# Attention with a conditioning token: other PSUM banks in the opening, and another order of sums, maxima and residual loads in the last two steps

## The chip, the cores and the metric

The kernel runs on one core of a Trainium2 chip. The metric is the device time of one execution in microseconds (us). TensorE multiplies matrices into PSUM, VectorE and ScalarE read PSUM, GpSimd works between tiles in SBUF, and the SP queue issues nearly all DMAs. PSUM has 8 banks of 128 x 512 float32 here, numbered 0 to 7.

## The reference, cut to what matters

```python
# x: (8, 512, 512), cond: (8, 512); 16 heads of 32
Q, K, V = heads(x @ Wq.T + bq), heads(x @ Wk.T + bk), heads(x @ Wv.T + bv)
tQ, tK  = heads(cond @ Wq.T + bq), heads(cond @ Wk.T + bk)
scores  = einsum('bhqd,bhkd->bhqk', Q + tQ, K + tK) / sqrt(32)
attn    = softmax(scores)
return x + einsum('bhqk,bhkd->bhqd', attn, V)      # heads put side by side again
```

All is float32. `x` comes back in as the residual; the bias of V is added to the residual, since the weights of a row sum to one.

## The kernel before, in words

The work is cut into T = 32 steps: step t is batch `t // 4` and a group of four heads `t % 4` (128 columns). Each step has four quarters. In quarter i of step t:

- `exponentials(t, i)` (L542) makes the scores of 128 keys by 512 queries for four heads, one bank each: first L547 puts minus the row maximum of each query in the bank, then L550 adds K times Q. ScalarE takes the exponential of each bank (L561) into tiles `es[t, i, pair]`.
- `row_max(t + 1, i + 1)` (L469) makes the scores of the next step the other way around, 128 queries by 512 keys (L486), for the row maxima on VectorE (L477 for one bank, L495 for two). `denominators` (L499) lets ScalarE run over the same banks once more (L505, tile `dead`) for the sums over keys. So such a bank comes free only when ScalarE is through with it.
- A third part differs by quarter: projections of a later batch (`project_pair`: `first_products`, `other_products`; L393 for q and k, L390 for v; seven products of half blocks in two banks, put together by VectorE at L431 to L447), or the product of the exponentials with V (`times_v`, L566, into one bank).

When all four quarters of maxima of a step are there, `split_max` (L513) has GpSimd cut them into three bfloat16 numbers (L519 to L522), and `transpose_max` (L526) turns those on TensorE (L531) and copies them out (L537, tile `maxT`), for the L547 of the next step.

The engines TensorE, ScalarE, VectorE and GpSimd issue their instructions in the order in which the program writes them (a schedule by hand). The SP queue alone is filled by a planner. Which banks a quarter uses is read from a table, `TURNS` (L83): each row is an order of the 8 banks. `banks(i)` is the i-th bank of the current row; `exponentials` takes places 0 to 3 and `row_max` places 4 to 7. `advance()` goes to the next row. Rows 0 to 7 serve the loop in turn, rows 8 to 11 steps 29 and 30 (`row(i)`), and rows 12 to 16 the opening (L716 to L737), where the maxima of step 0 and the first of step 1 are made between the projections of batch 0. Row 15 serves its quarter 3 of step 0 (`row_max(0, 3)`, `first_products("k", ...)` at places 3 and 2), row 16 the first quarter of step 1 (`row_max(1, 0)`, `transpose_max` at place 1, `other_products` at places 0 and 2).

Residuals: `load_residual(t)` (L153) loads a tile `xr` on SP, in four DMAs, and GpSimd adds the bias (L169). Tile `xr` has three buffers. For the last step the output is turned on TensorE, so its residual comes in another layout, in one DMA (L165), and before the change in the same three buffers. A buffer is free when `send` (L619) has used it: VectorE turns the product (L622), GpSimd multiplies by the reciprocals of the sums (L623) and adds the residual (L624), and SP writes out (L627).

Steps 29, 30 and 31 are written out after the loop. There is no projection left, so a product with V is made in pieces: `part_of` (L742) makes some quarters of it in a bank, ScalarE copies it out (L756, or L750 for later pieces), and GpSimd adds later pieces to the first (L751). Steps 30 and 31 have no `denominators`: their sums over keys are made from `es`. `sum_of` (L821) adds quarters 0 and 1 (L824) or one more quarter (L826) for one pair of heads, on VectorE or GpSimd, and `times_ones` (L574, L576) adds over the partitions on TensorE. `send_parts` (L764) takes the reciprocals (L766) and sends a step that was made in pieces.

Of the kernel before, what the change touches and what calls it, by code (L numbers as in the profile page):

```python
# [9 lines left out]
F32 = mybir.dt.float32  # L10
# [7 lines left out]
def kernel(  # L18
# [38 lines left out]
    nc = tc.nc  # L57
    P = 128
# [6 lines left out]
    NS = S // P  # L65
    NC = D // P
# [10 lines left out]
    op = ctx.enter_context(tc.tile_pool(name="op", bufs=2))  # L77
# [20 lines left out]
        (7, 4, 2, 3, 5, 6, 0, 1),  # L98
        (7, 4, 0, 1, 5, 6, 2, 3),
        (2, 3, 4, 7, 5, 6, 0, 1),  # L100
        (2, 3, 4, 7, 0, 1, 5, 6),
        (4, 7, 5, 6, 2, 3, 0, 1),
    ]
    turn = [0]

    def banks(i, n=1):

        j = TURNS[turn[0]][i]
        if n == 1:
            return psum[:, j, :]  # L110
        k = TURNS[turn[0]][i + 1]
        return psum[:, j : k + 1 : k - j, :]
# [19 lines left out]
    BL = 32  # L132
    NB = S // BL
# [13 lines left out]
    xr = {}  # L147
# [5 lines left out]
    def load_residual(t):  # L153

        b, g = divmod(t, G)
        if turned_by_vector(t):
            xr[t] = op.tile([P, NB, BL], F32, tag="xr", name=f"xr_{t}", bufs=3)
            for h in range(HG):
                nc.sync.dma_start(
                    xr[t][h * BL : (h + 1) * BL], spread(x[b], g * P + h * BL)  # L160
                )
            bias = bvs[:, g, :].unsqueeze(1).broadcast_to([P, NB, BL])
        else:
            xr[t] = op.tile([P, NS, P], F32, tag="xr", name=f"xr_{t}", bufs=3)
            nc.sync.dma_start(  # L165
                xr[t], x[b].rearrange("(c p) d -> p c d", p=P)[:, :, g * P : (g + 1) * P]
            )
            bias = bvb[:, g * P : (g + 1) * P].unsqueeze(1).broadcast_to([P, NS, P])
        nc.gpsimd.tensor_tensor(xr[t], xr[t], bias, ALU.add)  # L169
# [134 lines left out]
    def turn_x(n):  # L304
        b, cc = divmod(n, NC)
        if b >= B:
            return
        if cc == 0:
            xT[b] = xtp.tile([P, NC, S], F32, tag="xT", name=f"xT_{b}")
        nc.vector.transpose(xT[b][:, cc, :], xs[n].rearrange("p f i -> p (f i)"))  # L310
        load_block(n + NC)
# [157 lines left out]
    def row_max(t, qc):  # L469
        if t >= T:  # L470
            return
        open_max(t)
        for j in range(HG):
            row_scores(t, qc, j, banks(HG + j))
        if t < T - 2:
            for j in range(2):
                nc.vector.tensor_reduce(  # L477
                    nmax[t][:, qc, j : j + 1, 0], banks(HG + j), AX.X, ALU.max, negate=True
                )
        else:  # L480
            row_max_of(t, qc, 0, banks(HG, 2))
        row_max_of(t, qc, 1, banks(HG + 2, 2))
# [43 lines left out]
    def transpose_max(t, bank, copy=nc.vector.tensor_copy):  # L526
        if t >= T:
            return
        pt = bank.bitcast(BF16)
        for qc in range(NS):  # L530
            nc.tensor.transpose(  # L531
                pt[:, qc * P : (qc + 1) * P],
                split[t % 2][:, qc, :, :].rearrange("p h e -> p (h e)"),
                identb,
            )
        maxT[t] = op.tile([P, S], BF16, tag="maxT", name=f"maxT_{t}")
        copy(maxT[t], pt[:, :S])  # L537
# [36 lines left out]
    def times_ones(of, pt, start, stop):  # L574
        for j in range(HG):
            nc.tensor.matmul(  # L576
                pt[j * HD : (j + 1) * HD, :],
                ones[:, :HD],
                of[j // 2][:, j % 2, :],
                start=start,  # L580
                stop=stop,
            )
# [84 lines left out]
    def bank(i):  # L667
        return psum[:, i, :]
# [71 lines left out]
    parts = {}  # L740

    def part_of(t, pt, of, between=None):  # L742

        for k, kc in enumerate(of):
            if k and between:
                between()
            times_v(t, kc, pt, of)
        if t in parts:
            p = op.tile([P, S], F32, tag="dead", name=f"part_{t}_{of[0]}")
            nc.scalar.copy(p, pt)  # L750
            nc.gpsimd.tensor_tensor(parts[t], parts[t], p, ALU.add)  # L751
        else:
            if not parts:
                parts["all"] = stage.tile([P, NC, D], F32, tag="w", name="parts")
            parts[t] = parts["all"][:, t % NC, :]
            nc.scalar.copy(parts[t], pt)  # L756
# [7 lines left out]
    def send_parts(t, den):  # L764
        rec = op.tile([P, NB, 1], F32, tag="recs", name=f"recs_{t}")
        nc.vector.reciprocal(rec, den)  # L766
        send(t, parts[t], rec)

    for t in range(T - 3):
        b, r = divmod(t, G)  # L770

        exponentials(t, 0)
        row_max(t + 1, 1)
        of = ((t - 1) // G + 1, (t - 1) % G)
        dens = lambda: denominators(t + 1, 1)
        if t:
            project_pair("q", *of, dens, nothing, 1 if r % 2 else (0, 3))
        else:
            first_products("v", 0, 0, dens, nothing, 3)
            turn_x(NC + 2)  # L780
        turn_x(t + NC + 3)
        advance()

        exponentials(t, 1)
        row_max(t + 1, 2)
        dens = lambda: denominators(t + 1, 2)
        if t:
            dens()
            weighted(
                t - 1, banks(0), banks(1), lambda: combine_x(b + 1, r) if r < 2 else None  # L790
            )
        else:
            dens()
            other_products("v", 0, 0, nothing, nothing, (1, 0))
        advance()

        exponentials(t, 2)
        row_max(t + 1, 3)
        split_max(t + 1)
        dens = lambda: denominators(t + 1, 3)  # L800
        if t:
            project_pair("k", *of, dens, nothing, 1 if r % 2 else (0, 3))
        else:
            first_products("v", 0, 1, dens, nothing, 3)
            combine_x(1, 0)
        load_residual(t + 1)
        advance()

        exponentials(t, 3)
        row_max(t + 2, 0)  # L810
        dens = lambda: denominators(t + 2, 0)

        def small():
            transpose_max(t + 1, banks(2 if r % 2 else 1))

        project_pair("v", *of, dens, small, 1 if r % 2 else (0, 2))
        advance()
# [3 lines left out]
    def sum_of(t, to, kc, on, prs=range(NP)):  # L821
        for pr in prs:
            if kc == 1:
                on.tensor_tensor(to[pr], es[t, 0, pr], es[t, 1, pr], ALU.add)  # L824
            else:
                on.tensor_tensor(to[pr], to[pr], es[t, kc, pr], ALU.add)  # L826

    def room_for_sums(t):
        a = stage.tile([P, NC, D], F32, tag="w", name=f"acc_{t}")
        return [a[:, pr * 2 : pr * 2 + 2, :] for pr in range(NP)]  # L830

    def row(i):
        turn[0] = 8 + i

    t = T - 3
# [2 lines left out]
    row_max(t + 1, 1)  # L838
    part_of(t - 1, banks(0), [0, 1])
    load_residual(t + 1)  # L840
    row(1)
    exponentials(t, 1)
    row_max(t + 1, 2)
# [8 lines left out]
    den = denominators_of(t - 1, banks(1))  # L852
# [6 lines left out]
    t = T - 2  # L859
# [2 lines left out]
    row_max(t + 1, 1)  # L862
    apart = masked(t - 1)
    part_of(t - 1, banks(0), [2])
    load_residual(t + 1)
    row(1)
    exponentials(t, 1)
    row_max(t + 1, 2)
    part_of(t - 1, banks(0), [3])
    spread_sums(apart, banks(1))  # L870
    den = denominators_of(t - 1, banks(1))
    row(2)
    exponentials(t, 2)
    row_max(t + 1, 3)
    acc = room_for_sums(t)
    sum_of(t, acc, 1, nc.gpsimd, [0])
    split_max(t + 1)
    part_of(t, banks(0), [0])
    send_parts(t - 1, den)

    exponentials(t, 3, (1, 2, 3, 4))
    sum_of(t, acc, 1, nc.vector, [1])
    part_of(
        t, bank(5), [1, 2], lambda: transpose_max(t + 1, bank(0), nc.vector.tensor_copy)
    )
    sum_of(t, acc, 2, nc.vector)
    sum_of(t, acc, 3, nc.vector)

    t = T - 1
    exponentials(t, 0, (6, 7, 1, 2))  # L890
    part_of(t - 1, bank(3), [3])
    exponentials(t, 1, (0, 4, 5, 6))
    pv = bank(7)
    times_v(t, 0, pv)
    exponentials(t, 2, (1, 2, 3, 0))
    times_v(t, 1, pv)
    times_ones(acc, bank(4), True, True)
    den = parts["all"][:, t % NC, :].rearrange("p (f e) -> p f e", e=BL)
    acc2 = room_for_sums(t)
    sum_of(t, acc2, 1, nc.vector)  # L900
    nc.vector.transpose(den.rearrange("p f e -> p (f e)"), bank(4))
    send_parts(t - 1, den[:, :, 0:1])
    exponentials(t, 3, (5, 6, 1, 2))
    times_v(t, 2, pv)
    pd = bank(3)
    times_ones(acc2, pd, True, False)
    times_ones([es[t, 2, pr] for pr in range(NP)], pd, False, False)
    times_ones([es[t, 3, pr] for pr in range(NP)], pd, False, True)
# [5 lines left out]
    two = [slice(0, HS), slice(HS, S)]  # L914
    nc.vector.tensor_copy(oT[:, two[0]], pv[:, two[0]])
    nc.scalar.copy(oT[:, two[1]], pv[:, two[1]])
    pi, po = bank(0), [bank(5), bank(1)]
    untranspose(den, pi)
    rec = op.tile([P, NS, HG, 1], F32, tag="rec", name="rec")
    nc.vector.reciprocal(  # L920
# [52 lines left out]
```

## Time and profile before

| | |
|---|---|
| median of 3 runs | 741.74 us (741.56 to 742.1) |
| the profiled execution | 741.48 us |
| its span in the profile | 739.6 us |
| TensorE, matmuls | busy 729.2 us (99%) |
| ScalarE | 620.6 us (84%) |
| VectorE | 535.2 us (72%) |
| GpSimd | 185.3 us (25%) |
| granted TensorE clock | 0.998 |

The span runs from the first instruction to the last end; all times of the text are counted from its start. In a line of the timeline stand the start, the duration, the engine and line, what is written and read, and how many instructions were merged; brackets hold the idle time before and what ended it. PE is TensorE, ACT ScalarE, DVE VectorE, POOL GpSimd. In a list of waits stand the waiting engine and line, what it waited for, us in total, times, and the longest. A matmul that waits while others are in flight is shown as a longer busy time, not as idle time, so distances between starts tell more than busy time does.

### The profile page before, as it was taken

The page shows a single profiled execution, that of the slowest core. Times are in us where ns is not written, and L with a number is a line of the kernel's source. Part 1 is how long each engine was busy: PE and PEld are TensorE (multiplying, and loading weights), DVE is VectorE, ACT ScalarE, POOL GpSimd, SP SyncE. Part 2 cuts the span into 40 slices and gives each one's busy share as a digit, 9 for nine tenths or more (in the row PEclk, how much of TensorE's full clock was granted, in tenths as well). Part 3 has the DMA queues.
Part 4 walks back from the last instruction along what each step waited for, and adds up shares of the span by engine and source line. Part 5 has one row for each costly group of instructions (what it writes and reads, how often), then busy time and mean ns, then how long its engine had stood idle before and what let it go on. Part 6 is the DMA issues. An engine that isn't in the chain of part 4 may idle for free.

```text
span 739.6 us, 15126 instructions
## 1 busy us (share of the span) xinstructions
PE 729.2 (99%) x5432; PEld 406.5 (55%) x5432; DVE 535.2 (72%) x845; ACT 620.6 (84%) x1546; POOL 185.3 (25%) x283
## 2 busy tenths in 40 slices
PE   9999999999999999999999999999999999999987
PEld 6566555655555565555566555566555556555422
DVE  3588777777777876777776877677676776766776
ACT  2478888988988988988989898898898898898664
POOL 3721211222211122221122221122222112222273
PEclk9999999999999999999999999999999999999999
DMA  8511212222212212221222221222111011111012
GB/s 261 85 30 29 37 24 43 34 39 45 44 26 33 44 30 44 44 33 27 43 33 40 44 43 23 37 41 33 29 31 16 15 30 29 30 29 25 7 29 43
DMA packets 194270, 29.63 MB, mean 40 GB/s; under 512 B 190986, under 2 KB 192010, under 8 KB 194196
## 3 DMA queue, kind: packets, MB, share of 16 engines
q1 hardware_dynamic: 193616, 28.01, 22.6%
q8 instruction: 42, 0.69, 0.4%
q10 hardware_dynamic: 580, 0.68, 0.3%
q14 instruction: 32, 0.26, 0.1%
HBM read 20.27 MB, written 8.39 MB: 39 GB/s over the span
## 4 chain that ended last, share of the span: by engine, by line
PE 94%; POOL 1%; DVE 1%; ACT 1%; DMA 1%; issue 1%; SPq 0%; DVEq 0%; POOLq 0%; ACTq 0%
PE psum L393 25%; PE psum L566 15%; PE psum L486 15%; PE psum L550 14%; PE psum L390 14%; PE psum L547 6%; PE psum L337 2%; PE psum L531 1%; DVE nmax L495 1%; PE psum L253 1%; ACT e L561 1%; PE psum L576 1%; DMA x<-in_x_dram 1%; DMA xr<-in_x_dram 0%; PE psum L298 0%
## 5 line engine op out<-in xcount | busy, mean ns | idle before, releaser
L505 ACT ACTIVATE dead<-psum,nmax 128x512 f32<-128x512 f32 x480 | 326.9, 700 | 8.1 <-DVE nmax L477 5.4
L561 ACT ACTIVATE e<-psum 128x512 f32<-128x512 f32 x512 | 264.4, 604 | 76.5 <-PE psum L550 76.5
L477 DVE TENSOR_REDUCE nmax<-psum 128x1 f32<-128x512 f32 x240 | 154.7, 686 | 144.6 <-PE psum L486 144.6
L495 DVE TENSOR_REDUCE nmax<-psum 128x2 f32<-128x1024 f32 x136 | 164.7, 1216 | 10.4 <-PE psum L486 9.1
L623 POOL TENSOR_TENSOR res<-res,recs 128x512 f32<-128x512 f32 x31 | 32.4, 1047 | 443.5 <-DVE res L622 443.5
L486 PE MATMUL psum<-kT,qT 32*128 32x512 f32 x1024 | 137.2, 601 | 0.1
L550 PE MATMUL psum<-qT,kT 32*128 32x512 f32 x1024 | 133.0, 588 | 0.0
L566 PE MATMUL psum<-e,v 128*32 128x512 f32 x1024 | 120.8, 597 | 0.0
L505 ACT ACTIVATION_READ_ACCUMULATOR dead<-psum,nmax 128x1 f32 x480 | 104.6, 218 | 0.0
L486 PEld LDWEIGHTS psum<-kT,qT 32*128 32x128 f32 x1024 | 58.3, 183 | 57.0 <-ACT dead L505 20.6
L566 PEld LDWEIGHTS psum<-e,v 128*32 128x32 f32 x1024 | 26.4, 110 | 65.4 <-issue 37.0
L547 PE MATMUL psum<-maxT,onesb 3*128 3x512 bf16 x512 | 52.7, 384 | 0.3 <-ACT dead L505 0.3
L550 PEld LDWEIGHTS psum<-qT,kT 32*128 32x128 f32 x1024 | 51.1, 185 | 2.4 <-issue 0.2
L390 PE MATMUL psum<-wc_v,xc 128*128 128x256 f32 x192 | 49.5, 380 | 0.3 <-ACT e L561 0.2
L547 PEld LDWEIGHTS <-onesb 3*128 3x128 bf16 x512 | 13.5, 91 | 62.1 <-issue 52.5
L393 PE MATMUL psum<-xc,wc_q 128*128 128x256 f32 x180 | 46.2, 379 | 0.0
L393 PE MATMUL psum<-xc,wc_k 128*128 128x256 f32 x180 | 46.2, 379 | 0.0
L624 POOL TENSOR_TENSOR res<-res,xr 128x512 f32<-128x512 f32 x31 | 40.4, 1303 | 2.4
L169 POOL TENSOR_TENSOR xr<-xr,bvs 128x512 f32<-128x512 f32 x31 | 39.3, 1268 | 2.8 <-DMA xr<-in_x_dram 2.6
L390 PEld LDWEIGHTS psum<-wc_v,xc 128*128 128x128 f32 x192 | 36.3, 190 | 6.0 <-ACT e L561 1.1
L390 PE MATMUL psum<-wT_v,xT 128*128 128x256 f32 x128 | 38.7, 405 | 0.0
L393 PEld LDWEIGHTS psum<-xc,wc_q 128*128 128x128 f32 x180 | 34.2, 190 | 4.7
(156 smaller groups left out, 790.7 us busy)
## 6 DMA issues: line engine op xcount, KB each, us to landing
xr<-in_x_dram SPq DMA_DIRECT2D x124, 64.0 KB, 2.4
out_dram<-res SPq DMA_DIRECT2D x124, 64.0 KB, 2.0
x<-in_x_dram SPq DMA_DIRECT2D x112, 64.0 KB, 2.4
w_q<-in_L_cond_Wq_dram SPq DMA_DIRECT2D x4, 256.0 KB, 4.6
w_k<-in_L_cond_Wk_dram SPq DMA_DIRECT2D x4, 256.0 KB, 3.6
w_v<-in_L_cond_Wv_dram SPq DMA_DIRECT2D x4, 256.0 KB, 4.5
x<-in_x_dram ACTq DMA_DIRECT2D x2, 256.0 KB, 4.4
x<-in_x_dram SPq DMA_DIRECT2D x2, 256.0 KB
```

The source lines that it names most:

```text
L169: nc.gpsimd.tensor_tensor(xr[t], xr[t], bias, ALU.add)
L390: nc.tensor.matmul(pt, xb, w, start=(kc == kcs[0]), stop=(kc == kcs[-1]))
L393: nc.tensor.matmul(pt, w, xb, start=(kc == kcs[0]), stop=(kc == kcs[-1]))
L477: nc.vector.tensor_reduce(nmax[t][:, qc, j : j + 1, 0], banks(HG + j), AX.X, ALU.max, negate=True)
L486: nc.tensor.matmul(pt, qkT["q", t][r, qc * P : (qc + 1) * P], qkT["k", t][r, :], start=True, stop=True,)
L495: nc.vector.tensor_reduce(nmax[t][:, qc, pr * 2 : pr * 2 + 2, 0], pt, AX.X, ALU.max, negate=True)
L505: nc.scalar.activation(dead, banks(HG + j), AF.Exp, bias=nmax[t][:, qc, j, :], accum_out=sums[t][:, qc, j, :],)
L547: nc.tensor.matmul(bank[j], onesb[r, :], maxT[t][r, :], start=True, stop=False)
L550: nc.tensor.matmul(bank[j], qkT["k", t][r, kc * P : (kc + 1) * P], qkT["q", t][r, :], start=False, stop=True,)
L561: nc.scalar.activation(e[:, i, :], bank[pr * 2 + i], AF.Exp)
L566: nc.tensor.matmul(pt[j * HD : (j + 1) * HD, :], vs[b % 2][:, kc, (g * HG + j) * HD : (g * HG + j + 1) * HD], es[t, kc, j // 2][:, j % 2, ...
L624: nc.gpsimd.tensor_tensor(y, y, xr.pop(t), ALU.add)
```

## The change

- Rows 15 and 16 of `TURNS` name other banks.
- The residual of the last step has a buffer of its own (`xr_last`), and it is loaded in step 29's first quarter in place of step 30's. `load_residual(1)` is called in the first quarter of step 0 in place of its third.
- In step 30 the sum of quarters 0 and 1 is made for both pairs on GpSimd, right after the maxima of quarter 2 are under way; before, one pair was made on GpSimd ahead of the split of step 31's maxima, and the other on VectorE. The send of step 29 comes after the four later sums of step 30 on VectorE.
- Step 30's product with V stays in one bank (0) over all four quarters. The three pieces with their copies and additions are gone; `send` reads the bank, and the sums have a tile of their own in place of the pieces' tile.
- The banks of the last exponentials and of the last outputs are renumbered to keep bank 0 out of use.

```diff
-        (2, 3, 4, 7, 0, 1, 5, 6),
-        (4, 7, 5, 6, 2, 3, 0, 1),
+        (2, 3, 0, 1, 6, 7, 4, 5),
+        (4, 0, 5, 1, 2, 3, 6, 7),
...
-            xr[t] = op.tile([P, NS, P], F32, tag="xr", name=f"xr_{t}", bufs=3)
+            xr[t] = op.tile([P, NS, P], F32, tag="xr_last", name=f"xr_{t}", bufs=1)
...
             turn_x(NC + 2)
+            load_residual(1)
...
-        load_residual(t + 1)
+        if t:
+            load_residual(t + 1)
...
     load_residual(t + 1)
+    load_residual(t + 2)
     row(1)
...
     part_of(t - 1, banks(0), [2])
-    load_residual(t + 1)
     row(1)
     exponentials(t, 1)
     row_max(t + 1, 2)
+    acc = room_for_sums(t)
+    sum_of(t, acc, 1, nc.gpsimd)
     part_of(t - 1, banks(0), [3])
     spread_sums(apart, banks(1))
     den = denominators_of(t - 1, banks(1))
     row(2)
     exponentials(t, 2)
     row_max(t + 1, 3)
-    acc = room_for_sums(t)
-    sum_of(t, acc, 1, nc.gpsimd, [0])
     split_max(t + 1)
-    part_of(t, banks(0), [0])
+    pa = banks(0)
+    times_v(t, 0, pa)
+
+    exponentials(t, 3, (1, 2, 3, 4))
+    times_v(t, 1, pa)
+    transpose_max(t + 1, bank(5), nc.vector.tensor_copy)
+    times_v(t, 2, pa)
+    for kc in (2, 3):
+        sum_of(t, acc, kc, nc.vector)
     send_parts(t - 1, den)
-
-    exponentials(t, 3, (1, 2, 3, 4))
-    sum_of(t, acc, 1, nc.vector, [1])
-    part_of(
-        t, bank(5), [1, 2], lambda: transpose_max(t + 1, bank(0), nc.vector.tensor_copy)
-    )
-    sum_of(t, acc, 2, nc.vector)
-    sum_of(t, acc, 3, nc.vector)
 
     t = T - 1
     exponentials(t, 0, (6, 7, 1, 2))
-    part_of(t - 1, bank(3), [3])
-    exponentials(t, 1, (0, 4, 5, 6))
+    times_v(t - 1, 3, pa)
+    exponentials(t, 1, (3, 4, 5, 6))
     pv = bank(7)
     times_v(t, 0, pv)
-    exponentials(t, 2, (1, 2, 3, 0))
+    exponentials(t, 2, (1, 2, 3, 4))
     times_v(t, 1, pv)
-    times_ones(acc, bank(4), True, True)
-    den = parts["all"][:, t % NC, :].rearrange("p (f e) -> p f e", e=BL)
+    pd = bank(5)
+    times_ones(acc, pd, True, True)
     acc2 = room_for_sums(t)
     sum_of(t, acc2, 1, nc.vector)
-    nc.vector.transpose(den.rearrange("p f e -> p (f e)"), bank(4))
-    send_parts(t - 1, den[:, :, 0:1])
-    exponentials(t, 3, (5, 6, 1, 2))
+    den = op.tile([P, NB, BL], F32, tag="dead", name=f"den_{t - 1}")
+    nc.vector.transpose(den.rearrange("p f e -> p (f e)"), pd)
+    rec = op.tile([P, NB, 1], F32, tag="recs", name=f"recs_{t - 1}")
+    nc.vector.reciprocal(rec, den[:, :, 0:1])
+    send(t - 1, pa, rec)
+    exponentials(t, 3, (6, 1, 2, 3))
     times_v(t, 2, pv)
-    pd = bank(3)
+    pd = bank(4)
...
-    pi, po = bank(0), [bank(5), bank(1)]
+    pi, po = bank(2), [bank(6), bank(1)]
```

## The prediction

> **What bounds the kernel now.** I read the page's first part, then the chain that ended last, then TensorE's waits, and last the timelines of the opening and the end.
>
> ```profile
> PE   729.2 (99%) x5432; PEld 406.5 (55%) x5432; DVE 535.2 (72%) x845; ACT 620.6 (84%) x1546; POOL 185.3 (25%) x283
> PE 94%; POOL 1%; DVE 1%; ACT 1%; DMA 1%; issue 1%; SPq 0%; DVEq 0%; POOLq 0%; ACTq 0%
> ```
>
> TensorE is busy for 99% and makes 94% of the chain, so only what lets TensorE go earlier counts. But "busy" covers matmuls that stretch while they wait for a bank, so I compared the distances between groups of matmuls with the shortest distance of the same pair of groups. From 90 to 690 us nothing worth having is lost. Three places remain. The first, by TensorE's waits and the chain near the end:
>
> ```profile
> PE psum L531 <- POOL split L522: 2.9, 1, 2.9
> ...
> 707.62 3.07 DMA xr<-in_x_dram
> ...
> 710.83 1.28 POOL xr L169
> 712.11 1.23 POOL parts L751
> 713.34 2.32 POOL acc L824
> 715.66 1.20 POOL split L519
> ...
> 717.57 0.27 POOL split L522
> 717.84 0.05 issue
> 717.88 0.40 PE psum L531 x4
> ```
>
> To be seen: TensorE waits 2.9 us for step 31's split maxima. GpSimd did them late because, in one queue, it had first waited for the residual's DMA (3.48 us idle), then added the bias, a part and half a sum. The second place is eight microseconds later, in the timeline:
>
> ```profile
> 725.65 2.05 PE L576 MATMUL psum<-acc,ones 128*32 128x512 f32 x8
> 727.64 0.40 PE L547 MATMUL psum<-maxT,onesb 3*128 3x512 bf16 x4
> ...
> 718.73 7.87 DVE L826 TENSOR_TENSOR acc<-acc,e 128x1024 f32<-128x1024 f32 x4
> ...
> 721.04 4.48 POOL L751 TENSOR_TENSOR parts<-parts,part 128x512 f32<-128x512 f32 x2
> ```
>
> The sums over keys of step 30 end on VectorE at 726.60, and the products with ones need them from 725.65. The third place is the opening, in TensorE's timeline:
>
> ```profile
> 37.32 1.13 PE L393 MATMUL psum<-xc,wT_q 128*128 128x256 f32 x4
> ...
> 40.75 1.80 PE L486 MATMUL psum<-kT,qT 32*128 32x512 f32 x8
> 42.48 1.13 PE L393 MATMUL psum<-xT,wT_k 128*128 128x256 f32 x4
> ...
> 50.88 0.39 PE L547 MATMUL psum<-maxT,onesb 3*128 3x512 bf16 x2 [0.30 <-ACT dead L505]
> ```
>
> The eight score matmuls of `row_max(0, 3)` take 1.80 us where the quarters before took 1.14: they go to banks 0, 1, 5, 6, the very banks whose exponentials of quarter 2 ScalarE ends only at 38.9 to 41.3.
>
> **The change, part by part.** All times are on the clock of the profile before.
>
> Banks of the opening. Quarter 3's scores go to 6, 7, 4, 5. Bank 6 is given up by ScalarE at 39.5, 4 and 7 by VectorE at 36.8, 5 at 38.8, so nothing waits. From the products at 37.32 to the scores is 3.43 us against 3.22 in the quarter before (33.03 to 36.25): 0.21. From the scores to the next products is 1.73 (40.75 to 42.48) against 1.07 (36.25 to 37.32): 0.66. Later `exponentials(0, 0)` starts at 50.19 in banks 3, 0, 1, 2, and 1 is held by the last `dead` of quarter (1, 0), until 50.7; with the new rows that one is in bank 7, and 0 and 1 hold only the turned maxima and a finished product. From L547 to the scores at 51.84 is 1.66 us; in the next quarter 56.52 to 57.60, 1.09. That is 0.57. Sum 1.44. What follows must keep up: VectorE's maxima of (0, 3) start 1.16 us after their matmuls (31.96 to 33.12), so at 41.7 in place of 41.91, and the split ends at 45.5, before TensorE turns it at 45.9. Bank 0 of that turn is free once VectorE has read the product at 44.9. In t = 0 TensorE waits for ScalarE at 54.16, 58.94 and 65.56; those waits move along, since ScalarE's exponentials there start 1.28 us after their L547.
>
> `load_residual(1)` moves by half a step within t = 0: four DMAs and one GpSimd add. The DMAs go out anyway among twelve at 23.77 to 30.10 on SP. The add took 1.27 us at 67.93 and now stands behind that of residual 0 at 45.76, when GpSimd is idle until 66.79. It leaves the place where it met `combine_x`:
>
> ```profile
> L320 DVE TENSOR_TENSOR xc<-xT x7: 626/626/1379, 68.4 to 587.2; 128x512 f32<-128x512 f32 x7
> ```
>
> The one of 1379 ns is this one. VectorE gains up to 0.75, of which its next maxima, bound to matmuls at 69.00, can use 0.22. That is enough for L413, whose end at 74.66 held up one of four heads: 74.55 to 75.76 is 1.21 us against 0.95 nine microseconds earlier (63.25 to 64.20). Between 0 and 0.26; I take 0.2.
>
> The residual of step 31: one DMA (0.51 us of SP) and one add (1.28) go from step 30 to step 29, into a buffer of its own. With no buffer to wait for, SP can send it after 30.10, and SP is idle until 47.00. If it is sent only behind the four at 681.25 to 683.6, it lands by 687.2 (3.07 after issue), the add ends at 688.5, and GpSimd's next work is at 694.53. Cover of 6 us, so nothing; each us beyond would hold TensorE.
>
> The sums ahead of the split. Both halves of sum 1 now stand on GpSimd, at 2.37 each (row L824), before the add of step 29's last part (1.27) and the split (1.24, from 44.47 to 45.70). The exponentials that they need are there at 707.85 and 708.85. 707.9 + 2.32 + 2.32 + 1.25 is 713.8; the maxima come from VectorE at 713.87. So the split runs 713.93 to 715.17 and TensorE turns it at 715.2, not at 717.88: **2.67 us**. It was ready at 714.93, so 0.28 stays. GpSimd has 0.1 us to spare here; every tenth beyond is lost.
>
> One bank for step 30. Three ScalarE copies (0.58, 0.59, 0.62) and two GpSimd adds (4.48 together) vanish. The copies stood where ScalarE had room, but for 0.2 us at 722.7. The adds matter: with them gone, and the send of step 29 put behind the sums, GpSimd is idle while VectorE adds. A row tells what that is worth:
>
> ```profile
> L826 DVE TENSOR_TENSOR acc<-acc,e x4: 1215/2298/2299, 718.7 to 724.3; 128x1024 f32<-128x1024 f32 x4
> ```
>
> Alone 1215 ns, beside GpSimd 2299, while L751 went from 1265 to 2257. [...] I take no wait; the end of the range takes up to 0.5.
>
> TensorE from 715.2 with unstretched distances: L531 0.33, L566 1.00, then exponentials and product 1.18 + 1.00, 1.18 + 1.01, 1.18 + 0.88, and ones 0.98, which gives L547 of the last quarter at 723.9 in place of 727.64. **3.7 us**, of which 1.0 is the second place (725.65 to 727.64 is 1.99, against 0.98). From there to the end all is alike. The sends: step 29's from 713.8 to about 720.8, out of SP by 728; step 30's transpose by 727.5, GpSimd until 729.9, SP until 731.9; the last output now issues on SP at 732.4. Cover 0.5 us. The new banks of the last outputs (2, 6, 1) were given up by 727.3.
>
> **Sum.** 1.44 + 0.2 + 3.7 = 5.3. The profiled execution had a span of 739.6 and took 741.48, the median is 741.74. So span 734.3, and **736.4 us**.
>
> **Rivals.** A, as above: 736.4; its own range is 735.8 to 737.0. B: GpSimd and VectorE collide more than I allow, the split by 0.5 (GpSimd has 0.1 spare) or `acc2` by 0.5 to 1: 737.2. For it speaks the 1.26 us of the cast at 715.59 where others took 0.25; against, that VectorE reads PSUM alone at 707.9 to 713.9. C: the opening gives its 1.44 back to ScalarE, which at 84% paces t = 0: gain 3.9, 737.8. For it the three waits there; against, ScalarE's idle 0.7 to 1.2 us before each group of exponentials. D, slower: step 30's send, now behind `acc2`, holds SP's queue, and the final output waits for its four DMAs. Each us beyond the 0.5 of cover is one at the end; from 5.8 us late it is slower than before, 2 us worse 743.7. Nothing on that chain is so long: `acc2`, transposes and two adds are 7 us in all. E: the moved work was covered elsewhere and nothing shows, 741.7; only if SP sent the residual late again.
>
> **How the numbers follow.** A 0.62, B 0.18, C 0.13, D 0.04, E 0.03. The range of 8 in 10 reaches over A, B and C's near half: 735.7 to 737.9; its low end lets the 0.28 vanish and banks a little more. A measurement of this kernel tells 0.2%, 1.5 us, from no change; A, B and C are all faster by over that: 0.93. Slower is D, 0.04, same E, 0.03.
>
> **What would show it.** L531 waits under 0.5 us; L826 at about 1.2 us four times; the last L576 before L547 in about 1 us; L486 after 40.5 in 1.14; L547 at 49.3 unbroken; L320 never above 0.7. I am wrong if GpSimd's two sums end after 712.7, if `acc2` ends the wait of L576, or if TensorE gains its 1.4 us by 49 and has lost it by 76.

## The result, and the profile after

The changed kernel takes 736.49 us (median of 6 runs, 736.3 to 736.61), the kernel before 741.92 us (6 runs, 741.32 to 743.69; the three known before the forecast are among them). The ratio is 0.9922, with a 95% interval of 0.9912 to 0.9933: 5.8 us less, give or take 0.8; the two medians differ by 5.4. The profiled execution has a span of 734.3 us, 5.3 under the 739.6 of before. Forecast were 736.4 us and a span of 734.3.

The page of the changed kernel, its first part and its chain:

```profile
PE 726.8 (99%) x5432; PEld 405.7 (55%) x5432; DVE 530.0 (72%) x844; ACT 618.9 (84%) x1543; POOL 182.8 (25%) x282
PE 97%; ACT 1%; DVE 1%; DMA 1%; issue 0%; POOL 0%; DVEq 0%; POOLq 0%
```

TensorE now makes 97% of the chain, and GpSimd's share is down to nothing. What TensorE waits for, by the list of waits, and the chain at the split:

```profile
PE psum L531 <- POOL split L522: 0.2, 1, 0.2
```

```profile
709.67 2.35 DVE nmax L495 x2
712.02 0.05 issue
712.08 0.27 POOL split L519
...
713.04 0.27 POOL split L522
...
713.36 0.40 PE psum L531 x4
```

The wait for the split is 0.2 us where it was 2.9, and ahead of the split stand VectorE's maxima, no longer a DMA or a sum. The timeline of the changed kernel, the end on VectorE and TensorE:

```profile
714.14 4.62 DVE L828 TENSOR_TENSOR acc<-acc,e 128x1024 f32<-128x1024 f32 x4
719.41 3.18 DVE L826 TENSOR_TENSOR acc<-e,e 128x1024 f32<-128x1024 f32 x2
...
719.29 1.23 PE L550 MATMUL psum<-qT,kT 32*128 32x512 f32 x8
720.45 1.06 PE L566 MATMUL psum<-e,v 128*32 128x512 f32 x8
721.33 1.04 PE L576 MATMUL psum<-acc,ones 128*32 128x512 f32 x8
722.31 0.40 PE L547 MATMUL psum<-maxT,onesb 3*128 3x512 bf16 x4
```

The four sums of step 30 (L828; line numbers move by two here) take 4.62 us where they took 7.87, and the products with ones (L576) no longer wait: 0.97 us to the next group, where it was 1.99. One thing is new: L550 at 719.29 takes 1.16 us to the next group, 0.2 more than its neighbours. The opening, on TensorE:

```profile
40.32 1.14 PE L486 MATMUL psum<-kT,qT 32*128 32x512 f32 x8
41.39 1.13 PE L393 MATMUL psum<-xT,wT_k 128*128 128x256 f32 x4
...
49.09 0.40 PE L547 MATMUL psum<-maxT,onesb 3*128 3x512 bf16 x4
...
72.88 1.03 PE L486 MATMUL psum<-kT,qT 32*128 32x512 f32 x8
73.83 1.13 PE L393 MATMUL psum<-xT,wT_q 128*128 128x256 f32 x4
```

The scores of `row_max(0, 3)` take 1.14 us, L547 runs unbroken, and the scores of quarter (2, 1) at 72.88 are 0.95 us ahead of the next products, where it was 1.21.

To see where the 5.3 us come from, I compared starts of the same group of matmuls in the two profiles. The last product before the split, first before and then after the change:

```profile
713.95 1.06 PE L566 MATMUL psum<-e,v 128*32 128x512 f32 x8
```

```profile
712.09 1.06 PE L566 MATMUL psum<-e,v 128*32 128x512 f32 x8
```

At 36 us the changed kernel is 0.22 ahead (36.25 against 36.03; its first transposes ended sooner). That is chance and no part of the change: a kernel with the new rows alone, whose loads are those of before, stands there at 36.01. At the first products of quarter (2, 1) the changed kernel is 1.93 ahead (75.76 against 73.83), so the opening gave 1.71. At the last product before the split it is 1.86 ahead, so 0.07 is lost between. At L531 it is 4.52 ahead (717.88 against 713.36): 2.66 from the split. At the last quarter's L547 it is 5.33 ahead (727.64 against 722.31): 0.81 from the sums. From there to the end nothing changes.

### The profile page after: what moved, and what is told of

It is laid out like the page before. It is cut to its first block, busy times and chain, and to the rows that moved or that the text cites. A ratio compares the mean times of both kernels' runs of the same rounds, so it can differ in the third digit from the quotient of the medians.

```text
span 734.3 us, 15120 instructions
## 1 busy us (share of the span) xinstructions
PE 726.8 (99%) x5432; PEld 405.7 (55%) x5432; DVE 530.0 (72%) x844; ACT 618.9 (84%) x1543; POOL 182.8 (25%) x282
## 4 chain that ended last, share of the span: by engine, by line
PE 97%; ACT 1%; DVE 1%; DMA 1%; issue 0%; POOL 0%; DVEq 0%; POOLq 0%
PE psum L393 26%; PE psum L566 16%; PE psum L486 15%; PE psum L550 15%; PE psum L390 14%; PE psum L547 6%; PE psum L337 2%; PE psum L531 1%; PE psum L253 1%; ACT e L561 1%; DMA x<-in_x_dram 1%; PE psum L576 0%; PE psum L298 0%; DVE nmax L495 0%; PE psum L644 0%; PE psum L631 0%
## 5 line engine op out<-in xcount | busy, mean ns | idle before, releaser
L623 POOL TENSOR_TENSOR res<-res,recs 128x512 f32<-128x512 f32 x31 | 33.3, 1076 | 446.8 <-DVE res L622 446.8
L486 PE MATMUL psum<-kT,qT 32*128 32x512 f32 x1024 | 136.3, 601 | 0.0
L550 PE MATMUL psum<-qT,kT 32*128 32x512 f32 x1024 | 133.0, 589 | 0.0
L566 PE MATMUL psum<-e,v 128*32 128x512 f32 x1024 | 120.5, 597 | 0.0
L486 PEld LDWEIGHTS psum<-kT,qT 32*128 32x128 f32 x1024 | 57.7, 183 | 56.6 <-ACT dead L505 19.7
L566 PEld LDWEIGHTS psum<-e,v 128*32 128x32 f32 x1024 | 26.3, 110 | 65.2 <-issue 37.7
L547 PE MATMUL psum<-maxT,onesb 3*128 3x512 bf16 x512 | 52.6, 385 | 0.0
L550 PEld LDWEIGHTS psum<-qT,kT 32*128 32x128 f32 x1024 | 51.1, 186 | 2.4 <-issue 0.2
L547 PEld LDWEIGHTS <-onesb 3*128 3x128 bf16 x512 | 13.5, 91 | 61.5 <-issue 51.8
L624 POOL TENSOR_TENSOR res<-res,xr 128x512 f32<-128x512 f32 x31 | 40.4, 1302 | 2.4
```

Source lines behind the costliest of these rows:

```text
L486: nc.tensor.matmul(pt, qkT["q", t][r, qc * P : (qc + 1) * P], qkT["k", t][r, :], start=True, stop=True,)
L547: nc.tensor.matmul(bank[j], onesb[r, :], maxT[t][r, :], start=True, stop=False)
L550: nc.tensor.matmul(bank[j], qkT["k", t][r, kc * P : (kc + 1) * P], qkT["q", t][r, :], start=False, stop=True,)
L566: nc.tensor.matmul(pt[j * HD : (j + 1) * HD, :], vs[b % 2][:, kc, (g * HG + j) * HD : (g * HG + j + 1) * HD], es[t, kc, j // 2][:, j % 2, ...
L624: nc.gpsimd.tensor_tensor(y, y, xr.pop(t), ALU.add)
```

## The experiments

My theory: three waits of TensorE were shortened, each by the part of the change that stands beside it, and two of them by way of VectorE's sums and GpSimd's operations, which last longer beside each other: in the kernel before a sum (L826) takes 1.22 us alone and 2.30 beside GpSimd. The rivals: ScalarE takes the opening's gain back; the order of the sums or the load alone is the gain; what stands beside the sums plays no part.

**The rows of the opening alone**, in the kernel before:

```diff
-        (2, 3, 4, 7, 0, 1, 5, 6),
-        (4, 7, 5, 6, 2, 3, 0, 1),
+        (2, 3, 0, 1, 6, 7, 4, 5),
+        (4, 0, 5, 1, 2, 3, 6, 7),
```

> The kernel before with the two rows of TURNS for the opening alone. My theory (the banks of the opening cost 1.44 us, which nothing takes back): the scores of row_max(0, 3) take 1.14 us in place of 1.80, L547 of the first exponentials is unbroken, and the time falls by 1.4 us, to 740.4; the end of the kernel keeps its wait of 2.9 us for L522. Rival C (ScalarE paces step 0): the opening is earlier by 1.4 us at 49 us and later again by 76 us, and the time falls by less than 0.5 us. If moving residual 1 also belongs to the gain before 76 us, the stretched L486 of quarter (2, 1) is still there (1.28 us).

Measured: 740.55 us (8 runs, 739.87 to 741.92), ratio to the kernel before 0.9975 (0.9965 to 0.9985), 1.8 us less. From the scores of (0, 2) to the products of quarter (2, 1) are 38.07 us (from 36.01 to 74.08) in place of 39.51: 1.44 less, and all of it is kept at 74 us. Rival C falls. The stretched L486 of quarter (2, 1) is still there, in the timeline of this kernel:

```profile
72.86 1.29 PE L486 MATMUL psum<-kT,qT 32*128 32x512 f32 x8
74.08 1.13 PE L393 MATMUL psum<-xT,wT_q 128*128 128x256 f32 x4
```

The surprise is at the end. Its profiled execution took 741.92 us, 2 us more than its best. The timeline around the split, which here waits as long as before:

```profile
716.43 0.61 PE L531 MATMUL psum<-identb,split 128*128 128x128 bf16 x4 [2.89 <-POOL split L522]
716.97 1.94 PE L566 MATMUL psum<-e,v 128*32 128x512 f32 x8
```

A product with V that takes 1.06 us elsewhere takes 1.94 here. Stretches of the same execution; the third figure from the end is the granted clock:

```profile
708.00:712.00 4.00, 4.00 (x38) 1.20 (x32) 2.77 (x3) 2.85 (x7) 2.64 (x3) 1.00 0.15 46
712.00:716.00 4.00, 1.54 (x16) 0.16 (x8) 3.28 (x4) 2.06 (x4) 3.86 (x4) 0.98 0.00 0
716.00:720.00 4.00, 3.57 (x20) 1.21 (x24) 2.86 (x3) 0.59 (x1) 2.84 (x5) 0.50 0.11 18
720.00:722.00 2.00, 2.00 (x16) 0.20 (x8) 2.00 (x2) 0.82 (x2) 2.00 (x1) 0.50 0.61 90
722.00:724.00 2.00, 2.00 (x20) 0.41 (x12) 2.00 (x2) 1.72 (x4) 0.17 (x2) 0.84 0.09 14
724.00:728.00 4.00, 4.00 (x40) 1.02 (x36) 2.64 (x3) 3.77 (x8) 1.39 (x1) 1.00 0.00 0
```

TensorE is granted half its clock from the last part of the wait on: the means of 0.98 to 716, 0.50 to 722 and 0.84 to 724 make 6.8 us of 0.50. In the profile of the kernel before, with a wait of 2.87 us, the clock stayed at 1.00 there. So the wait that the change took away seems to have a second price, paid in some executions only. The run with the filled wait below tests it.

**The early load alone**, in the kernel before:

```diff
-            xr[t] = op.tile([P, NS, P], F32, tag="xr", name=f"xr_{t}", bufs=3)
+            xr[t] = op.tile([P, NS, P], F32, tag="xr_last", name=f"xr_{t}", bufs=1)
...
     load_residual(t + 1)
+    load_residual(t + 2)
...
     part_of(t - 1, banks(0), [2])
-    load_residual(t + 1)
```

> The kernel before with the residual of step 31 in its own buffer and loaded in step 29, and nothing else. GpSimd then idles no more for the DMA, so the half sum is made before VectorE's maxima end. [...] Rival (the sum ahead of the split was the cause): wait still over 2.5 us, no gain.

Measured: 739.7 us (5 runs, 739.62 to 739.75), ratio 0.9961 (0.9949 to 0.9974). TensorE waits 1.21 us for the split. The timeline of this kernel, TensorE, GpSimd and VectorE:

```profile
716.21 0.40 PE L531 MATMUL psum<-identb,split 128*128 128x128 bf16 x4 [1.21 <-POOL split L522]
...
714.25 0.24 POOL L520 TENSOR_TENSOR rest<-nmax,split 128x16 f32<-128x16 f32 x1
714.55 1.25 POOL L521 CAST split<-rest 128x16 bf16<-128x16 f32 x1
...
714.50 1.18 DVE L824 TENSOR_TENSOR acc<-e,e 128x1024 f32<-128x1024 f32 x1
```

The third operation of the split stands for 1.25 us in place of 0.25, for just as long as VectorE's sum of two tiles runs, and the sum, at 1.18 us, is not slowed. So the load gives 1.66 us of the wait, and the sum on VectorE holds back 1.0 of the rest. The time fell by more than 1.66: the medians differ by 2.6. The five runs lie within 0.13 us of each other at a mean granted clock of 0.998 to 1.000, where those of the kernel before beside them have 0.995 to 0.998; a half clock that no longer comes would account for the difference, but it was not taken apart.

**The changed kernel without the early load**:

```diff
-            xr[t] = op.tile([P, NS, P], F32, tag="xr_last", name=f"xr_{t}", bufs=1)
+            xr[t] = op.tile([P, NS, P], F32, tag="xr", name=f"xr_{t}", bufs=3)
...
     load_residual(t + 1)
-    load_residual(t + 2)
...
     part_of(t - 1, banks(0), [2])
+    load_residual(t + 1)
```

> The changed kernel with the residual of step 31 loaded where it was before: in step 30's first quarter, into one of the three shared buffers. GpSimd waits for it until about 708.9 on this kernel's clock, and now both half sums, the last part and the split stand behind it: 708.9 + 1.28 + 1.27 + 4.7 + 1.27 + 1.24 = 718.7 for the split, where the changed kernel has 713.3. Theory (the new order of the sums is only worth something with the early load): wait of L531 about 5.4 us, the time up by 5 us to 741.6, about the kernel before. Rival (the order of the sums is the gain and the load is a detail): up by less than 1.5 us.

Measured: 742.97 us (11 runs, 741.73 to 743.52), ratio to the kernel before 1.0002 (0.9993 to 1.0011): the whole gain is gone. The wait list and GpSimd's timeline:

```profile
PE psum L531 <- POOL split L522: 4.2, 1, 4.2
```

```profile
709.74 1.28 POOL L169 TENSOR_TENSOR xr<-xr,bvb 128x512 f32<-128x512 f32 x1 [3.47 <-DMA xr<-in_x_dram]
710.97 4.67 POOL L826 TENSOR_TENSOR acc<-e,e 128x1024 f32<-128x1024 f32 x2
715.59 1.27 POOL L751 TENSOR_TENSOR parts<-parts,part 128x512 f32<-128x512 f32 x1
```

With two half sums behind the DMA instead of one, the split is done at 718.03, and TensorE waits 4.16 us, longer than in the kernel before. The 5.4 us that I expected were too much: my sum has the last part (L751, 1.27 us) in it twice, and GpSimd makes it once. On top comes the half clock in this profile (means of 0.68 from 716 to 718 us, 0.50 to 722 and 0.61 to 724): L566 after L531 takes 1.87 us to the next group, not 1.00. The new order of sums is worth something only with the load.

**The product of step 30 in pieces again, and the send of step 29 ahead of the sums**, in the changed kernel (not shown: the other banks of steps 30 and 31, which go back too):

```diff
-    pa = banks(0)
-    times_v(t, 0, pa)
+    part_of(t, banks(0), [0])
+    send_parts(t - 1, den)
...
-    times_v(t, 1, pa)
-    transpose_max(t + 1, bank(5), nc.vector.tensor_copy)
-    times_v(t, 2, pa)
+    part_of(
+        t, bank(5), [1, 2], lambda: transpose_max(t + 1, bank(0), nc.vector.tensor_copy)
+    )
...
-    send_parts(t - 1, den)
...
-    times_v(t - 1, 3, pa)
-    exponentials(t, 1, (3, 4, 5, 6))
+    part_of(t - 1, bank(3), [3])
+    exponentials(t, 1, (0, 4, 5, 6))
...
-    exponentials(t, 2, (1, 2, 3, 4))
+    exponentials(t, 2, (1, 2, 3, 0))
```

> The changed kernel with step 30's product with V in three pieces again, its ScalarE copies and GpSimd additions, and the send of step 29 ahead of the sums, as in the kernel before; opening, load and the order of split and sums as changed. [...] At least two of the four L826 sums take about 2.3 us in place of 1.2. Rival (the sums were late for their late start alone): sums of 1.2 us, no wait, 736.5; then the three copies are off the path too. The 0.2 us which the changed kernel loses at L550 of step 31's third group is expected to go if bank 4 behind ScalarE is its cause, since bank 0 is in its place here.

Measured: 737.05 us (736.95 to 737.22), 0.6 above the changed kernel in its first runs, 0.4 above it in the last ones below. The sums, by their line, then GpSimd and TensorE:

```profile
L828 DVE TENSOR_TENSOR acc<-acc,e x4: 1215/2296/2302, 714.4 to 720.0; 128x1024 f32<-128x1024 f32 x4
```

```profile
714.58 2.21 POOL L624 TENSOR_TENSOR res<-res,xr 128x512 f32<-128x512 f32 x1
716.75 4.48 POOL L751 TENSOR_TENSOR parts<-parts,part 128x512 f32<-128x512 f32 x2
...
719.52 1.03 PE L550 MATMUL psum<-qT,kT 32*128 32x512 f32 x8
720.48 1.33 PE L566 MATMUL psum<-e,v 128*32 128x512 f32 x8
721.36 2.05 PE L576 MATMUL psum<-acc,ones 128*32 128x512 f32 x8
```

Three of the four sums are at 2.3 us again, beside GpSimd's L624 (the send of step 29, which this run also puts ahead of the sums) and its two additions. L576 stretches to 1.98 us, and from L531 to the last L547 are 9.75 us in place of 8.95: 0.80. L550 takes 0.96 to the next group. So the single bank and the later send together are worth 1.0 by way of the sums; what each gives alone was not measured. The new banks cost 0.2 at L550: with bank 0 kept for the product, the fourth bank of that group is bank 4, which ScalarE reads in the changed kernel until 719.23, while L547 for the group begins at 719.07.

**A half sum beside the split**, in the changed kernel:

```diff
-    sum_of(t, acc, 1, nc.gpsimd)
+    sum_of(t, acc, 1, nc.gpsimd, [0])
...
+    sum_of(t, acc, 1, nc.vector, [1])
     split_max(t + 1)
```

> The changed kernel, but the second half of sum 1 of step 30 is made by VectorE right after its last maxima, so beside the split; GpSimd makes the first half alone. Theory (a VectorE sum with two SBUF inputs and GpSimd exclude each other for a whole instruction): GpSimd has 2.3 us more room, and still the split is later, since one of its four operations is held for about 1 us: 1.25 us in place of 0.25; TensorE's wait for L522 rises from 0.20 to about 1.2 us, and the time by 1.0 us, to 737.5. Rival (GpSimd is simply slow, and any work taken from it helps): wait 0.2 us or less, time 736.5 or less.

Measured: TensorE waits 1.13 us. TensorE, GpSimd and VectorE in the timeline:

```profile
715.88 0.40 PE L531 MATMUL psum<-identb,split 128*128 128x128 bf16 x4 [1.13 <-POOL split L522]
...
713.67 1.18 POOL L519 CAST split<-nmax 128x16 bf16<-128x16 f32 x1 [2.40 <-DVE nmax L495]
...
713.52 1.22 DVE L826 TENSOR_TENSOR acc<-e,e 128x1024 f32<-128x1024 f32 x1
```

Here it is the first operation of the split that stands for 1.18 us, where it takes 0.26 in the changed kernel; the sum began 0.15 us sooner than it and takes 1.22, as it does alone. GpSimd had been idle for 2.4 us before, so work taken from it didn't help. From the product to L531 are 2.19 us in place of 1.27, 0.92 more. The time, 737.97 us (4 runs, 737.22 to 738.76), also holds a later start: in the profiled execution the scores of (0, 2) begin at 37.47, not at 36.03.

**Residual 1 in its old place**, in the changed kernel:

```diff
             turn_x(NC + 2)
-            load_residual(1)
...
-        if t:
-            load_residual(t + 1)
+        load_residual(t + 1)
```

> The changed kernel with load_residual(1) in step 0's third quarter again. Theory: the add L169 meets combine_x once more, L320 takes 1.38 us in place of 0.68, L413 ends some 0.2 us later, one head of the scores L486 of quarter (2, 1) waits, and the distance from that L486 to the next L393 is 1.21 to 1.22 us in place of 0.95: time up by 0.27 us, to 736.8. Rival (the bank rows alone did it): distance 0.95 us, time unchanged.

Measured: 737.05 us (4 runs, 737.02 to 738.19). The sum of `combine_x` and the scores, by line and timeline:

```profile
L320 DVE TENSOR_TENSOR xc<-xT x7: 626/628/1393, 68.1 to 587.1; 128x512 f32<-128x512 f32 x7
```

```profile
74.25 1.29 PE L486 MATMUL psum<-kT,qT 32*128 32x512 f32 x8
75.47 1.13 PE L393 MATMUL psum<-xT,wT_q 128*128 128x256 f32 x4
```

1.39 us is back (the changed kernel's longest is 0.68), and the distance is 1.22 in place of 0.95: 0.27. So the opening's 1.71 is 1.44 of banks and 0.27 of this. The median rose by 0.4 to 0.6, more than 0.27; it can't show so little, since the profiled execution also starts later here (scores of (0, 2) at 37.40).

**The wait filled with useless matmuls**, in the kernel before:

```diff
-    part_of(
-        t, bank(5), [1, 2], lambda: transpose_max(t + 1, bank(0), nc.vector.tensor_copy)
-    )
+    def fill_and_turn():
+        for _ in range(40):
+            nc.tensor.matmul(bank(7)[:, :P], onesb, onesb, start=True, stop=True)
+        transpose_max(t + 1, bank(0), nc.vector.tensor_copy)
+
+    part_of(t, bank(5), [1, 2], fill_and_turn)
```

> The kernel before with 40 matmuls of ones (128 x 128, results unused) that TensorE makes into bank 7 while it waits for step 31's split; all else is as before, so useless work is added. Theory (a wait of 2.9 us lets TensorE's clock drop to half for 6.8 us in some executions, as in the profile of the kernel with the new rows alone): the wait is cut to about 0.8 us by the filling, the clock stays at 1.0 behind it, and the times come close together, at 741.3 to 741.7, with none of 742.0 to 743.5 as the kernel before has on this chip; median 0.6 to 0.8 us under the kernel before on the same chip. Rival (the spread has nothing to do with this wait): the same spread of 2 us and the same median, or slower.

Measured: 741.54 us. Ten executions lie from 741.41 to 741.87 (an eleventh, of 1883.66, stands apart and is set aside); the kernel before on the same chip has a median of 742.38 and 15 executions from 741.64 to 743.41. Ratio 0.9989 (0.9979 to 0.9998). In the timeline:

```profile
715.26 2.41 PE L885 MATMUL psum<-onesb 128*128 128x128 bf16 x40
718.20 0.40 PE L531 MATMUL psum<-identb,split 128*128 128x128 bf16 x4 [0.53 <-POOL split L522]
718.53 1.06 PE L566 MATMUL psum<-e,v 128*32 128x512 f32 x8
```

Nothing became earlier: L531 still comes when GpSimd is done. The work added is 2.4 us, and yet the median falls by 0.84 (0.15 to 1.6 by the interval of the ratio). The lower clock is not seen here: the profile shows 1.00 behind the wait, and the mean granted clock of the ten is 0.998 to 1.000, that of the 15 beside them 0.995 to 0.998, the lowest in the slowest. That was the second price of the wait.

**More banks**, in the changed kernel, with the bank lists of steps 29 to 31 renumbered throughout (shown are the rows of step 29; three more, for step 30, are added to `TURNS`, and the banks named in steps 30 and 31 change too):

```diff
-        (6, 7, 0, 1, 2, 3, 4, 5),
-        (0, 1, 2, 3, 4, 5, 6, 7),
-        (2, 3, 4, 5, 6, 7, 0, 1),
+        (5, 6, 0, 7, 1, 4, 2, 3),
+        (6, 0, 1, 7, 4, 5, 2, 3),
+        (1, 4, 5, 7, 0, 6, 2, 3),
...
-        if t < T - 2:
+        if t < T:
...
-            first_products("v", 0, 0, dens, nothing, 3)
+            first_products("v", 0, 0, dens, nothing, 1)
...
-            first_products("v", 0, 1, dens, nothing, 3)
+            first_products("v", 0, 1, dens, nothing, 1)
```

> The changed kernel, with the same thought on banks carried on. In step 0 the second bank of first_products is that of the second exponential in place of the fourth, so it comes free 1 us sooner: two waits of 0.39 us go. In steps 29 and 30 the rows of banks are renumbered so that at most one of the four banks of a group of exponentials comes free late, and the first two maxima of a quarter are reduced one by one, so that a bank comes free 0.5 us sooner: of 0.55 us lost in each of four quarters and 0.36 in a fifth, 0.3 or more should go in each, against 0.14 us for two reductions in place of one ahead of the split. Together 1.5 to 2 us, time 734.5 to 735.0. Rival (ScalarE and VectorE pace these quarters, whatever the banks): less than 0.5 us.

Measured: 735.14 us (4 runs, 735.03 to 735.25), ratio to the kernel before 0.9904 (0.989 to 0.9917), just above the range expected. Both waits of 0.39 us in step 0 are gone. In steps 29 and 30 less went than I thought. The second quarter of step 30 in the timeline of this kernel:

```profile
702.73 0.73 PE L550 MATMUL psum<-maxT,onesb 3*128 3x512 bf16 x4
703.09 1.23 PE L553 MATMUL psum<-qT,kT 32*128 32x512 f32 x8
704.06 1.38 PE L489 MATMUL psum<-kT,qT 32*128 32x512 f32 x8
705.37 1.07 PE L569 MATMUL psum<-e,v 128*32 128x512 f32 x8
```

Three lines are added above, so L489 is what was L486. The exponentials' matmuls are 0.2 us sooner, and the scores behind them stretch to 1.38 us, since they now come before VectorE has given up two of their banks, at 704.26. From the first line to the last it is 2.64 us, as before (2.60). In the third quarters 0.31 goes. Ahead of the split 0.32 is added: TensorE waits 0.52 us in place of 0.20. The longer reductions are not the cause: VectorE's maxima end at 710.97, but GpSimd ends its sums and the last part only at 711.33, and the split follows at once. The tenth of a microsecond of room that GpSimd had is used up. There the rival was right in part: other engines pace these quarters, here GpSimd.

The two side by side on one chip:

> The changed kernel itself, on the same chip as the next, so that all three are compared side by side. 736.3 to 736.6 us, or a few tenths more where the first loads land later; no spread of over 0.5 us but from the start, since TensorE nowhere waits as long as 2.9 us.

> The kernel with more banks renumbered once more, beside the changed kernel. From its trace: two waits of 0.39 us gone in step 0, 0.31 gone in each of two quarters and 0.21 in a third, and 0.28 more at the split, together 1.33 us less than the changed kernel: 735.1 us where that has 736.5.

Measured: the kernel before 741.73 us (9 runs, 741.01 to 743.5), the changed kernel 736.64 (5 runs, 736.44 to 737.62; ratio 0.9935, 0.9921 to 0.9948), the one with more banks 734.89 (4 runs, 734.8 to 735.06; ratio 0.9908, 0.9894 to 0.9921). It beats both. The runs of the changed kernel spread over 1.2 us, more than expected; only the fastest of them has a profile, so whether the start did it is not shown. In the two profiles the scores of (0, 2) stand at 36.05 and 36.03, and the last quarter's L547 at 722.34 and 721.05: 1.29 us, where 1.33 were expected. The other 0.4 falls after that, where the banks of the last outputs changed too; this was not taken apart.

## Why the prediction was right, point by point

*The banks of the opening, 1.44.* Measured 1.44, by the rows alone and by the comparison of starts. None of it came back in step 0.

*Residual 1, 0.2 out of 0 to 0.26.* The upper end was true, 0.27: VectorE was early enough for the last head to go with the others.

*The residual of step 31 covered.* SP sent it at 47.85 us, behind a block of x and not at 30, and GpSimd had no DMA to wait for in step 30.

*The sums ahead of the split, 2.67.* Measured 2.66. GpSimd finished its two half sums and the last part at 711.99 and VectorE its maxima at 712.02, so the 0.1 us of room was hardly there at all, and it was enough; GpSimd's two sums ended at 710.76, which is 712.62 on the clock of before, where the prediction set its sign of being wrong at 712.7. The run without the load shows that this step stands on the one before it, the run with a half sum on VectorE that it stands on what VectorE does beside the split (L519 at 1.18 us in place of 0.26).

*The second place, 1.0.* This is the term that was mis-sized: measured 0.81. That the sums would be ready for L576 with GpSimd idle was an estimate; they took 4.62 us from first start to last end, each at about 1.2 us, as a lone one, and L576 lost its wait. But in the row of "unstretched distances" I put 1.18 for the third group of exponentials, and its banks 3 and 4 are the first two of the group before: it waits for ScalarE, 0.2 us. The pieces with bank 0 in that place don't have the wait.

*`acc2` beside the send.* No run shows the wait of up to 0.5 us that the end of the range held: the sums were done at 722.59, and TensorE asked at 724.37. The two sums took 3.18 us, between two lone ones (2.4 us, at 1.21 each) and two beside GpSimd (4.6, at 2.30 each): the first was not slowed (1183 ns), the second was (2074). GpSimd beside them:

```profile
719.57 1.94 POOL L623 TENSOR_TENSOR res<-res,recs 128x512 f32<-128x512 f32 x1 [6.26 <-DVE res L622]
721.59 2.13 POOL L624 TENSOR_TENSOR res<-res,xr 128x512 f32<-128x512 f32 x1
```

They went by turns: the first sum (from 719.41) began ahead of L623, which stands for 1.94 us where it takes 1.05 alone; the second sum then waited for L623, and L624 for the second sum. The other meetings looked at show the like: L521 took 1.25 us in place of 0.25 (the early load alone), L519 1.18 in place of 0.26 (the half sum on VectorE), L828 2.30 in place of 1.22 (the pieces), L320 1.39 in place of 0.63 (residual 1 in its old place). The maxima from PSUM, 2.36 us for two beside GpSimd's sums as ever, were not touched.

*The sends.* Step 30's was out of SP by 728.6, the last output issued at 730.78: 2.2 us of cover where 0.5 was forecast, for the most part since `acc2` came 1.4 us sooner than two sums of 2.30 us would have. Rival D was never near.

*The sum.* That the span of 734.3 was met to the tenth is luck. Without the 0.22 us of the start the parts measured make 5.1 (1.71, less 0.07, 2.66 and 0.81), where 5.3 was forecast; the chance at the start made good the 0.2 lost at L550.

*The list of places.* The prediction found three places worth having. There were more: the kernel with more banks took its further 1.75 us (medians) in step 0, in steps 29 and 30 and at the very end.

*What the prediction left out* is the clock. Its sum was made against a profiled execution in which the clock was 1.00 behind the wait, and so it gave the right span; but the median of before holds some executions with a lower mean clock (0.995 to 0.998 beside the filled wait, against 0.998 to 1.000 with it). The filled wait puts that at 0.84 us in the median, with an interval of 0.15 to 1.6. That the ratio says 5.8 where the profiles say 5.3 agrees with it; chance in the start is as large, so this was not taken apart further.

## What to carry to other kernels

When an engine with a queue in order does small urgent work (here four operations of 0.25 us), look at everything that stands ahead of it in the queue and at what the engine beside it runs (here one such operation stood for 1.18 to 1.25 us beside a sum on VectorE): a DMA wait for data needed much later, or a sum made too early, is paid for by the engine that waits at the end. Move the load first, then the order; the order without the load made the wait longer (4.16 us for 2.87). And compare distances between starts of the same groups: of the 5.3 us, only 2.7 for the split and 0.3 for L547 stood in the list of waits.

## What the runs showed of the hardware that was not expected

Behind a wait of TensorE of 2.9 us half its clock was lost, in two of the profiles. From the start of the last matmul before it to the start of the next it is 3.5 us. With 2.87 us the profile of before shows 1.00 from 700 to 733 us, with 2.89 us that of the rows alone shows 0.50 for 6.8 us, with 4.16 us that of the kernel without the load shows it too, for 6.8 us; with 1.13 us (the half sum on VectorE, mean clock 1.000) and 1.21 us (the early load alone, 1.00 from 700 to 733) it was not seen.

The length of the wait alone doesn't tell who lost the clock, since 2.87 us kept it and 2.89 lost it. By the means of the stretches, half a clock began at 715.8 in the profile of the rows alone, where TensorE had been idle since 713.54, for 2.3 us, and at 716.7 in that without the load, after 2.8 us idle. In the kernel before TensorE was idle for 2.87 us and the clock stayed. What else decides is not shown, and three profiles are few.

The start varies by more than 1 us from execution to execution: the first 16 transposes took 2.50 us in the profile of the changed kernel and 3.64 in that with residual 1 in its old place, and the scores of (0, 2) begin at 36.03 in the one and at 37.40 in the other. The record of the clock may point to why. It begins with the full clock at 5.80 us in the changed kernel and at 6.70 in the kernel before, where the transposes took 2.91 us. What the clock was before is not recorded, but 28 matmuls of 128x128 at the very start take 3.17 us, 113 ns each, and 40 of the same shape in the filled wait 2.41, 60 each. No run changed the start on purpose, and two profiles are few, so this is agreement and not a test. For every comparison of a few tenths it is chance, which is why those were made between starts of groups within a profile.
